# Gate product on GpSimd, second normalization on ScalarE as scale and bias

## The chip, the cores and the metric

The kernel runs on one core of one Trainium2 chip. The metric is device time in microseconds (us). Before the change it is 3508.47 us, the median of three runs (3508.07 to 3510.55).

A core has several engines, each with its own in-order instruction queue: TensorE (PE in the profile; its weight loads are listed as PEld), VectorE (DVE), ScalarE (ACT), GpSimd (POOL) and SyncE (SP), which here only issues DMAs. They meet only at semaphores. SBUF is the on-chip memory, PSUM the small memory that TensorE writes to.

## What is computed

The input x has 8 batches of 2048 positions with 512 channels, all in 32-bit floats. Cut to what matters:

```python
def _layernorm(x, axis=-1, eps=1e-05):
    m = jnp.mean(x, axis=axis, keepdims=True)
    v = jnp.var(x, axis=axis, keepdims=True)
    return (x - m) / jnp.sqrt(v + eps)

def attn(x):                       # a gated long convolution
    proj = (x @ in_proj_w + in_proj_b).reshape(B, L, C, 3)
    v = short_conv(proj[..., 0]) + short_b
    h = coefs(pos)                 # a small network gives the filter, as long as the sequence
    conv = irfft(rfft(v, n=2 * L) * rfft(h, n=2 * L), n=2 * L)[:, :L]
    return (proj[..., 2] * conv) @ out_w + out_b

def ffn(x):                        # 8 chosen adapters, mixed
    return einsum('k,kod,bsd->bso', weights, W[ids], x) + einsum('k,ko->o', weights, b[ids])

x = x + attn(_layernorm(x))
x = x + ffn(_layernorm(x))
```

The reference loops over two convolution branches, but only the last one reaches the output, so the kernel computes that one.

## The kernel before, in words

The Fourier transform over a sequence is split in two: across the 128 partitions it is a matrix product with a table, and across the 16 positions that a partition holds it is a second, small product. This gives three stages.

1. The first stage (lines 330 to 382) normalizes x, projects it to v and to the gate x2, transforms v across the partitions and stores both to DRAM. The adapters are mixed and the filter is built (lines 175 to 327) between its batches.
2. The middle stage (lines 385 to 440) goes over 32 groups of frequencies: it finishes the transform, multiplies by the filter and starts the way back. GpSimd adds the complex products at lines 426 and 427.
3. The last stage (lines 443 to 501) is where the change lies. It loops over 8 groups n of two position rows and, inside, over 8 batches b: 64 iterations, with two tiles t of 128 x 512 in each.

One iteration of the last stage, with the line of each step:

- SP loads zt (460, the transformed convolution), x2 (462, the gate; its tile is named x2t) and xt (464, the block's input). Each has three buffers.
- For each of the two tiles, GpSimd makes cor (468 and 469, a correction term, two instructions) and xb (471, the input plus the output bias). TensorE ends the inverse transform in ps_y (474, two matmuls). VectorE adds cor (479) and multiplies by the gate (480), both into gt. TensorE transposes gt in four pieces (166), ScalarE copies the result to gT (167), TensorE projects it with out_w into ps_o (171, four matmuls), and VectorE adds xb and has x1 (485).
- `layer_norm_stats` (144 to 153) makes mean and 1/sd of both tiles: two bn_stats (148), two bn_aggr (150), one Sqrt on ScalarE (152), one reciprocal (153). `normalized` (155 to 160) makes xn1 on VectorE, one instruction for each tile, subtracting the mean and multiplying by 1/sd (157).
- For each tile, TensorE transposes xn1 (166), ScalarE copies it to xn1T (167), GpSimd adds the adapters' bias to x1 for x1b (495), TensorE projects with mixed_wT (171) and VectorE adds x1b into ot (498). GpSimd issues the store of both (499).

Because helpers record their own lines, L166, L167 and L171 each stand for two places; the tile names tell them apart. In the timeline xn1 appears as xn, and x1 as x. Each 32-bit matmul leaves two records in the trace.

The source order is not the order of the queues. The tile framework's scheduler fixes each engine's order when the kernel is built, taking an instruction when its inputs and a free buffer are there. The tiles gt, gT, cor, xb, x1, xn1, xn1T, x1b and ot have two buffers each, the pools ps_x and ps_y two banks each and ps_o four. So the stage is pipelined over iterations. In the trace TensorE's steady order is: the adapter projection of one iteration, the transposes of gt and the output projection of the next, the ps_y of a still later one, and then the transposes of xn1. VectorE has, in the steady state: ot for the first tile, ot for the second, two of L479, two of L480, then x1, bn_stats and bn_aggr for each tile, the reciprocal, two of L157. GpSimd has: the store's issue, four cor instructions, then x1b, xb, x1b, xb.

Of the kernel before, what the change touches and what calls it, by code (L numbers as in the profile page):

```python
# [25 lines left out]
F32 = mybir.dt.float32  # L26
I32 = mybir.dt.int32
AF = mybir.ActivationFunctionType
ALU = mybir.AluOpType
# [3 lines left out]
P = 128  # L33
# [38 lines left out]
def block_kernel(  # L72
# [24 lines left out]
    nc = tc.nc  # L97
# [46 lines left out]
    def layer_norm_stats(pool, xt, to, n):  # L144

        bn = pool.tile([P, n, 6], F32, name="bn")
        for t in range(n):
            nc.vector.bn_stats(bn[:, t, :], xt[:, t, :])  # L148
        for t in range(n):
            nc.vector.bn_aggr(to[:, t, :], bn[:, t, :])  # L150
        sd = pool.tile([P, n], F32, name="sd")
        nc.scalar.activation(sd, to[:, :, 1], AF.Sqrt, bias=eps)  # L152
        nc.vector.reciprocal(to[:, :, 1], sd)  # L153

    def normalized(xn, xt, st, n):
        for t in range(n):
            nc.vector.tensor_scalar(  # L157
                xn[:, t, :], xt[:, t, :], st[:, t, 0:1], st[:, t, 1:2],
                ALU.subtract, ALU.mult,
            )  # L160

    def transposed(psum, src, to):

        ps = psum.tile([P, CC, P], F32, name="ps_t")
        for cc in range(CC):
            nc.tensor.transpose(ps[:, cc, :], src[:, ts(cc, P)], ident)  # L166
        nc.scalar.copy(to, ps)  # L167

    def projected(ps, xT, w):
        for kc in range(CC):  # L170
            nc.tensor.matmul(  # L171
                ps, lhsT=xT[:, kc, :], rhs=w[:, kc, :], start=(kc == 0), stop=(kc == CC - 1)
            )
# [156 lines left out]
    NR = 4  # L330
    with tc.tile_pool(name="vw", bufs=1) as vw, tc.tile_pool(
        name="vin", bufs=3
    ) as vin, tc.tile_pool(name="v2", bufs=2) as v2, tc.tile_pool(
        name="ps_a", bufs=2, space=PSUM
    ) as ps_a, tc.tile_pool(name="ps_b", bufs=3, space=PSUM) as ps_b, tc.tile_pool(
        name="ps_c", bufs=3, space=PSUM
# [13 lines left out]
        for b in range(B):  # L350
# [4 lines left out]
            for n in range(R // NR):  # L355
# [6 lines left out]
                x2 = v2.tile([P, NR, C], F32, name="x2")  # L362
# [23 lines left out]
    with tc.tile_pool(name="mt", bufs=3) as mt, tc.tile_pool(name="mh", bufs=2) as mh, tc.tile_pool(  # L386
        name="my", bufs=3
    ) as my, tc.tile_pool(name="ps_v", bufs=2, space=PSUM) as ps_v, tc.tile_pool(
        name="ps_z", bufs=4, space=PSUM
# [53 lines left out]
    NR = 2  # L443
    with tc.tile_pool(name="ofix", bufs=2) as ofix, tc.tile_pool(
        name="oin", bufs=3
    ) as oin, tc.tile_pool(name="o2", bufs=2) as o2, tc.tile_pool(
        name="ps_x", bufs=2, space=PSUM
    ) as ps_x, tc.tile_pool(name="ps_y", bufs=2, space=PSUM) as ps_y, tc.tile_pool(
        name="ps_o", bufs=4, space=PSUM
    ) as ps_o:  # L450
        ow_s = ofix.tile([P, CC, C], F32, name="ow_s", bufs=1)
        nc.sync.dma_start(ow_s, out_w.rearrange("(kc p) c -> p kc c", p=P))
        v0_b = ofix.tile([P, B, C], F32, name="v0_b", bufs=1)
        nc.sync.dma_start(v0_b, v0_d.partition_broadcast(P))
        for n in range(R // NR):
            fix = ofix.tile([P, 2, NR, C], F32, name="fix2")
            nc.sync.dma_start(fix, fix_d[:, :, ts(n, NR), :].rearrange("k p r c -> p k r c"))
            for b in range(B):
                zt = oin.tile([P, NR, 2, C], F32, name="zt")
                nc.sync.dma_start(zt, z_d[b, :, ts(n, NR), :, :])  # L460
                x2 = oin.tile([P, NR, C], F32, name="x2t")
                nc.sync.dma_start(x2, x2_d[b, :, ts(n, NR), :])
                xt = oin.tile([P, NR, C], F32, name="xt3")
                nc.sync.dma_start(xt, x[b].rearrange("(p r) c -> p r c", r=R)[:, ts(n, NR), :])
                x1 = o2.tile([P, NR, C], F32, name="x1")
                for t in range(NR):
                    cor = o2.tile([P, C], F32, name="cor")
                    nc.gpsimd.tensor_tensor(cor, fix[:, 0, t, :], v0_b[:, b, :], ALU.mult)
                    nc.gpsimd.tensor_tensor(cor, cor, fix[:, 1, t, :], ALU.add)
                    xb = o2.tile([P, C], F32, name="xb")  # L470
                    nc.gpsimd.tensor_tensor(xb, xt[:, t, :], out_bb, ALU.add)
                    ps = ps_y.tile([P, C], F32, name="ps_y")
                    for i in range(2):
                        nc.tensor.matmul(  # L474
                            ps, lhsT=last[:, i, :], rhs=zt[:, t, i, :],
                            start=(i == 0), stop=(i == 1),
                        )
                    gt = o2.tile([P, C], F32, name="gt")
                    nc.vector.tensor_tensor(gt, ps, cor, ALU.add)  # L479
                    nc.vector.tensor_tensor(gt, gt, x2[:, t, :], ALU.mult)  # L480
                    gT = o2.tile([P, CC, P], F32, name="gT")
                    transposed(ps_x, gt, gT)
                    ps = ps_o.tile([P, C], F32, name="ps_o")
                    projected(ps, gT, ow_s)
                    nc.vector.tensor_tensor(x1[:, t, :], ps, xb, ALU.add)  # L485
                st1 = o2.tile([P, NR, 2], F32, name="st1")
                layer_norm_stats(o2, x1, st1, NR)
                xn1 = o2.tile([P, NR, C], F32, name="xn1")
                normalized(xn1, x1, st1, NR)
                ot = o2.tile([P, NR, C], F32, name="ot")  # L490
                for t in range(NR):
                    xn1T = o2.tile([P, CC, P], F32, name="xn1T")
                    transposed(ps_x, xn1[:, t, :], xn1T)
                    x1b = o2.tile([P, C], F32, name="x1b")
                    nc.gpsimd.tensor_tensor(x1b, x1[:, t, :], mixed_bb, ALU.add)  # L495
                    ps = ps_o.tile([P, C], F32, name="ps_o")
                    projected(ps, xn1T, mixed_wT)
                    nc.vector.tensor_tensor(ot[:, t, :], ps, x1b, ALU.add)  # L498
                nc.gpsimd.dma_start(  # L499
                    out[b].rearrange("(p r) c -> p r c", r=R)[:, ts(n, NR), :], ot  # L500
                )
# [53 lines left out]
```

## Time and profile before

| | |
|---|---|
| median of three runs | 3508.47 us |
| the profiled execution's own time | 3511.88 us |
| its span, first to last instruction | 3510.1 us |
| mean granted TensorE clock | 0.974 |
| PE busy in the span | 3152.2 us (90%) |
| DVE busy | 1636.5 us (47%) |
| POOL busy | 1119.1 us (32%) |
| ACT busy | 592.7 us (17%) |
| last stage, first cor to the end | about 2110 to 3510 us |

A line of a group in the profile reads: source line, engine, operation, tile written <- tiles read, shapes, count | busy us in total, mean ns of one | idle us of the engine before it, and what released it. A line of the timeline reads: start in us, length in us, engine, line, operation, tiles, count of merged instructions, and in brackets the idle time before it with its releaser. A matmul's end is modelled; its start is recorded.

Over 200 us from the middle of the last stage (2800 to 3000 us), PE was busy 180.72 us, DVE 128.64, POOL 99.17 and ACT 24.33.

### The profile page before, as it was taken

How to read it: one execution, taken by the hardware profiler on the slowest of the kernel's cores; microseconds unless marked ns; L12 is line 12 of the kernel's file. 1: busy time of each engine (PE TensorE's matmuls, PEld its weight loads, DVE VectorE, ACT ScalarE, POOL GpSimd, SP SyncE). 2: the span in 40 equal slices, each digit the busy share in tenths (PEclk: the TensorE clock that was granted, in tenths of full speed). 3: DMA queues.
4: the chain of work that ended last, by engine and by line, in shares of the span. 5: the costliest groups of instructions: out<-in, count | busy, mean ns of one | idle time of the engine just before them, and what ended most of it. 6: DMA issues, size and time to landing. Idle time of an engine off the chain costs nothing. (4 is left out here: it accounts for less than half of the span.)

```text
span 3510.1 us, 25679 instructions
## 1 busy us (share of the span) xinstructions
PE 3152.2 (90%) x9142; PEld 1338.9 (38%) x9142; DVE 1636.5 (47%) x2225; ACT 592.7 (17%) x1110; POOL 1119.1 (32%) x934
## 2 busy tenths in 40 slices
PE   7999679999999998888888868999899999999997
PEld 3443124444444443222222214444444444444443
DVE  6222642222222211444444435666666666666663
ACT  1212111111111111222222221111111111111111
POOL 0000840000000000444444435455544444455542
PEclk9998669999999999999999999999999999999999
DMA  7322232223222223666666645333333333333330
GB/s 268 123 107 90 102 120 114 111 111 120 114 115 107 102 96 125 225 214 213 216 218 216 214 174 215 132 123 135 120 133 126 140 123 132 120 137 121 120 108 24
DMA packets 156119, 493.54 MB, mean 141 GB/s; under 512 B 11783, under 2 KB 16200, under 8 KB 139481
## 3 DMA queue, kind: packets, MB, share of 16 engines
q1 hardware_dynamic: 88312, 304.46, 24.8%
q10 hardware_dynamic: 56160, 145.50, 10.9%
q0 software_dynamic: 11520, 41.95, 3.0%
q8 instruction: 73, 1.20, 0.1%
q14 instruction: 54, 0.43, 0.0%
HBM read 273.75 MB, written 218.12 MB: 140 GB/s over the span
## 5 line engine op out<-in xcount | busy, mean ns | idle before, releaser
L426 POOL TENSOR_TENSOR y<-m 128x512 f32<-128x512 f32 x128 | 162.2, 1267 | 1288.5 <-DMA hs<-sh_d 917.9
L171 PE MATMUL ps_p<-wv_s,xnT 128*128 128x512 f32 x1024 | 469.9, 602 | 18.0 <-ACT xnT L167 18.0
L171 PE MATMUL ps_o<-ow_s,gT 128*128 128x512 f32 x1024 | 456.8, 599 | 18.7 <-ACT gT L167 18.7
L171 PE MATMUL ps_p<-wx_s,xnT 128*128 128x512 f32 x1024 | 460.3, 592 | 0.0
L171 PE MATMUL ps_o<-mixed_wT,xn1T 128*128 128x512 f32 x1024 | 454.6, 597 | 0.0
L432 PE MATMUL ps_z<-y,tab 64*128 64x512 f32 x1024 | 290.4, 644 | 89.3 <-POOL y L426 72.5
L480 DVE TENSOR_TENSOR gt<-gt,x2t 128x512 f32<-128x512 f32 x128 | 364.6, 2885 | 0.1
L370 DVE TENSOR_TENSOR v<-ps_p,bv_b 128x512 f32<-128x512 f32 x128 | 88.5, 691 | 468.6 <-PE ps_p L171 468.6
L378 ACT COPY s<-ps_s 128x512 f32<-128x512 f32 x256 | 149.9, 585 | 917.7 <-PE ps_s L377 917.7
L498 DVE TENSOR_TENSOR ot<-ps_o,x1b 128x512 f32<-128x512 f32 x128 | 88.6, 692 | 459.3 <-issue 273.5
L415 PE MATMUL ps_v<-s,tab 128*64 128x512 f32 x1024 | 280.8, 598 | 10.2 <-PE ps_v L415 10.2
L171 PEld LDWEIGHTS ps_p<-wx_s,xnT 128*128 128x128 f32 x1024 | 194.6, 190 | 244.9 <-issue 244.9
L171 PEld LDWEIGHTS ps_p<-wv_s,xnT 128*128 128x128 f32 x1024 | 190.3, 191 | 248.9 <-issue 215.3
L171 PEld LDWEIGHTS ps_o<-ow_s,gT 128*128 128x128 f32 x1024 | 189.2, 190 | 248.9 <-issue 213.8
L171 PEld LDWEIGHTS ps_o<-mixed_wT,xn1T 128*128 128x128 f32 x1024 | 191.3, 192 | 218.0 <-issue 217.4
L166 PE MATMUL ps_t<-ident,xn 128*128 128x128 f32 x1024 | 150.4, 281 | 128.1 <-DVE xn L157 127.9
L474 PE MATMUL ps_y<-zt,last 128*128 128x512 f32 x512 | 233.6, 599 | 21.2 <-DMA zt<-z_d 21.2
L377 PE MATMUL ps_s<-v,first 128*128 128x512 f32 x512 | 240.8, 592 | 0.0
L499 POOL DMA_DIRECT2D out<-ot x64 | 38.1, 595 | 585.1 <-DVE ot L498 585.1
L437 ACT COPY z<-ps_z 128x512 f32<-128x512 f32 x256 | 137.5, 589 | 505.5 <-PE ps_z L432 505.5
L421 DVE TENSOR_TENSOR m<-ps_v,h 128x512 f32<-128x512 f32 x128 | 87.9, 686 | 276.7 <-PE ps_v L415 276.7
L373 DVE TENSOR_TENSOR x<-ps_p,bx_b 128x512 f32<-128x512 f32 x128 | 88.4, 690 | 265.0 <-PE ps_p L171 264.5
(89 smaller groups left out, 3102.4 us busy)
## 6 DMA issues: line engine op xcount, KB each, us to landing
s_d<-s ACTq DMA_DIRECT2D x128, 512.0 KB
s<-s_d SPq DMA_DIRECT2D x64, 1024.0 KB
z_d<-z ACTq DMA_DIRECT2D x64, 1024.0 KB
zt<-z_d SPq DMA_DIRECT2D x64, 1024.0 KB
xt<-in_x SPq DMA_DIRECT2D x32, 1024.0 KB
x_d<-x SPq DMA_DIRECT2D x32, 1024.0 KB
x2t<-x_d SPq DMA_DIRECT2D x64, 512.0 KB
xt<-in_x SPq DMA_DIRECT2D x64, 512.0 KB
```

Of the source, the lines that this page charges most:

```text
L166: nc.tensor.transpose(ps[:, cc, :], src[:, ts(cc, P)], ident)
L171: nc.tensor.matmul(ps, lhsT=xT[:, kc, :], rhs=w[:, kc, :], start=(kc == 0), stop=(kc == CC - 1))
L370: nc.vector.tensor_tensor(v, ps, bv_b, ALU.add)
L377: nc.tensor.matmul(ps, lhsT=first[:, i, :], rhs=v, start=True, stop=True)
L378: nc.scalar.copy(s[:, i, :], ps)
L415: nc.tensor.matmul(ps[i][a * 64 : a * 64 + 64, :], lhsT=tab[:, ts(i, 64)], rhs=s[:, 2 * w + a, :], start=True, stop=True,)
L426: nc.gpsimd.tensor_tensor(y[:, 0, :], m[:, 0, :], m[:, 1, :], ALU.subtract)
L432: nc.tensor.matmul(pz[a], lhsT=tab[rows, ds(128 + 128 * i, P)], rhs=y[rows, i, :], start=(i == 0), stop=(i == 1),)
L437: nc.scalar.copy(z[:, 2 * w + a, :], pz[a])
L474: nc.tensor.matmul(ps, lhsT=last[:, i, :], rhs=zt[:, t, i, :], start=(i == 0), stop=(i == 1),)
L480: nc.vector.tensor_tensor(gt, gt, x2[:, t, :], ALU.mult)
L498: nc.vector.tensor_tensor(ot[:, t, :], ps, x1b, ALU.add)
```

## The change

The gate product of L480 is issued on GpSimd instead of VectorE, with the same operands. The call of `normalized` in the last stage is replaced: VectorE computes nb, which is minus mean times 1/sd, for both tiles in one instruction on [128, 2] operands, and ScalarE makes xn1 as Identity(x1 * scale + bias), with 1/sd as scale and nb as bias, one instruction for each tile. The first stage's normalization stays on VectorE.

```diff
                     gt = o2.tile([P, C], F32, name="gt")
                     nc.vector.tensor_tensor(gt, ps, cor, ALU.add)
-                    nc.vector.tensor_tensor(gt, gt, x2[:, t, :], ALU.mult)
+                    nc.gpsimd.tensor_tensor(gt, gt, x2[:, t, :], ALU.mult)
                     gT = o2.tile([P, CC, P], F32, name="gT")
...
                 xn1 = o2.tile([P, NR, C], F32, name="xn1")
-                normalized(xn1, x1, st1, NR)
+
+                nb = o2.tile([P, NR], F32, name="nb")
+                nc.vector.scalar_tensor_tensor(
+                    nb, st1[:, :, 0], -1.0, st1[:, :, 1], ALU.mult, ALU.mult
+                )
+                for t in range(NR):
+                    nc.scalar.activation(
+                        xn1[:, t, :], x1[:, t, :], AF.Identity, bias=nb[:, t : t + 1],
+                        scale=st1[:, t, 1:2],
+                    )
                 ot = o2.tile([P, NR, C], F32, name="ot")
```

## The prediction, made before the result was known

> **What bounds the kernel now.** I read the page's first part (PE busy 90% of the span), then the costliest groups for what PE waits for, then the timeline of one steady iteration of the last stage, engine by engine.
>
> From the groups, the gate product and the transposes of the normalized tiles (the last line covers the first stage too; in the list of waits, 106.9 of the 127.9 us fall between 2120 and 3470 us):
>
> ```profile
> L480 DVE TENSOR_TENSOR gt<-gt,x2t 128x512 f32<-128x512 f32 x128 | 364.6, 2885 | 0.1
> L166 PE MATMUL ps_t<-ident,xn 128*128 128x128 f32 x1024 | 150.4, 281 | 128.1 <-DVE xn L157 127.9
> ```
>
> TensorE's timeline over one iteration:
>
> ```profile
> 2812.52 7.13 PE L171 MATMUL ps_o<-ow_s,gT 128*128 128x512 f32 x16 [0.29 <-ACT gT L167]
> 2819.49 3.60 PE L474 MATMUL ps_y<-zt,last 128*128 128x512 f32 x8
> 2823.98 0.63 PE L166 MATMUL ps_t<-ident,xn 128*128 128x128 f32 x4 [0.89 <-DVE xn L157]
> 2825.39 0.63 PE L166 MATMUL ps_t<-ident,xn 128*128 128x128 f32 x4 [0.78 <-DVE xn L157]
> 2825.85 7.03 PE L171 MATMUL ps_o<-mixed_wT,xn1T 128*128 128x512 f32 x16
> ```
>
> The next transposes of gt start at 2832.72, those of this iteration started at 2811.19: a period of 21.53 us, of which PE idles 0.29 + 0.89 + 0.78 = 1.96. All but the 0.29 is waiting for VectorE's normalization. That is the only place where the last stage can be shortened without taking matmuls away: at most 1.67 us an iteration, 107 us in 64.
>
> VectorE and GpSimd in the same iteration:
>
> ```profile
> 2813.27 5.88 DVE L480 TENSOR_TENSOR gt<-gt,x2t 128x512 f32<-128x512 f32 x2
> 2819.07 0.68 DVE L485 TENSOR_TENSOR x<-ps_o,xb 128x512 f32<-128x512 f32 x1
> 2820.61 0.67 DVE L485 TENSOR_TENSOR x<-ps_o,xb 128x512 f32<-128x512 f32 x1
> 2822.59 0.17 DVE L153 RECIPROCAL st<-sd 128x2 f32<-128x2 f32 x1 [0.36 <-ACT sd L152]
> 2822.80 2.44 DVE L157 TENSOR_SCALAR xn<-x,st 128x512 f32<-128x512 f32 x2
> ```
>
> ```profile
> 2812.45 0.59 POOL L499 DMA_DIRECT2D out<-ot  x1 [9.02 <-DVE ot L498]
> 2813.07 2.49 POOL L468 TENSOR_TENSOR cor<-fix,v_b 128x512 f32<-128x512 f32 x2
> 2815.52 2.47 POOL L469 TENSOR_TENSOR cor<-cor,fix 128x512 f32<-128x512 f32 x2
> 2819.83 1.27 POOL L495 TENSOR_TENSOR x1b<-x,mixed_bb 128x512 f32<-128x512 f32 x1 [1.84 <-DVE x L485]
> 2823.50 1.45 POOL L471 TENSOR_TENSOR xb<-xt,out_bb 128x512 f32<-128x512 f32 x1
> ```
>
> The gate product is the thing to look at. Its least duration is 0.675 us, but the first of each pair took 5.28 (2813.27 to 2818.55) and the second about 0.6. GpSimd's four cor instructions ran from 2813.07 to 2817.99: a VectorE instruction with both inputs in SBUF stood still until GpSimd's whole run was over, then took 0.56. VectorE's additions with one input in PSUM (0.68), the statistics (0.69) and the reciprocal (0.17) show no such wait beside a busy GpSimd.
>
> **Part one: the gate product leaves VectorE.** Its 5.88 us go. They delayed the first x1 to 2819.07, although its half of the projection was done near 2816.0 (half of the 6.97 us from 2812.52); with its statistics it then pushed the second x1 to 2820.61, 1.1 us after the projection's end at 2819.49. Without it the second x1 starts one hop after that end. The chain that ended last has this hop and the rest undisturbed: PE ends 3465.39, DVE x starts 3465.48, the reciprocal ends 3467.66, so 2.18 us from x1 to the reciprocal's end. In the shown iteration: 2819.49 + 0.09 + 2.18 = 2821.76, where it was 2822.76. Gain: 1.0 us of the chain.
>
> On GpSimd it costs two instructions of 1.225 us (the spacing of cor: 2813.07 to 2814.30). The Trainium skill (GPSIMD Engine Reference, § Engine selection) speaks against it: elementwise with two inputs is about twice as slow there. The row agrees on the ratio (1.225 against 0.675) but that isn't what decides: by the rule the move loses 2 x 0.55 us, by the row it takes 5.88 us off VectorE and needs 2.45 of GpSimd, which idles about 9 us before each store. The product's result is not needed before the next transposes of gt at 2832.72, so the 2.45 us lie beside other work: nothing on the path directly. Queued behind it on GpSimd are cor (needed 20 us later), x1b (needed near 2829) and xb (needed an iteration later): all have slack. SP's reload of x2t starts earlier (its buffer is free at 2815.5, not 2819.15); the reload of xt, and zt behind it, starts 0.4 us later, with three buffers each. I cost these at nothing.
>
> What it does change is GpSimd's run. All its work of an iteration becomes ready near 2813 or soon after: two products, four cor, and x1b and xb twice, whose x1 now come at about 2816.7 and 2820.3. Ten instructions of 1.225 us from 2813.07 end at 2825.35, without a gap, where before there was a pause from 2817.99 to 2819.83. The order among the ten doesn't change this, unless one whose x1 is still missing is placed too early; cor stood ahead of x1b before, which speaks against that.
>
> **Part two: nb.** This is one tiny VectorE instruction, and it has two SBUF inputs. The trace has no tiny one of this kind. From below it is bounded by the reciprocal on 128x2, 0.17 us; from above by the gate product, waiting until GpSimd's run ends. It would be ready at 2821.79, in the middle of the new run. Both ways of waiting are in this trace. In the filter stage (L310 has two SBUF inputs as well) and in the last stage's first iteration:
>
> ```profile
> 423.44 1.74 DVE L310 TENSOR_TENSOR g<-hp,w_b 128x512 f32<-128x512 f32 x1 [1.15 <-POOL g L312]
> 429.99 4.17 DVE L310 TENSOR_TENSOR g<-hp,w_b 128x512 f32<-128x512 f32 x1 [1.48 <-POOL g L312]
> 2124.64 1.76 DVE L480 TENSOR_TENSOR gt<-gt,x2t 128x512 f32<-128x512 f32 x1
> ```
>
> The 1.7 us cases waited for one GpSimd instruction and then got in; the 4.17 us case sat out three. What tells them apart in the timeline: where GpSimd's run followed directly on a DMA that GpSimd issued (the store before cor; the filter's store before the run at 428.68), VectorE got in only when the run was over. Where GpSimd had stood idle for another engine (421.84), or had issued no DMA (2124.64), it got in after one. The new run follows directly on the store's issue at 2812.45, just as the cor run does. So I take the upper end: nb ends about 0.1 us after the run, at 2825.45, instead of 2821.97.
>
> Here the Trainium skill differs from the row: SBUF — State Buffer, § Who interferes with whom and the summary's last rows, says that a VectorE instruction with two SBUF inputs contends with a reading GpSimd instruction, and that the second to issue blocks until the first finishes. By the rule nb waits for one instruction, to 2822.87 (2813.07 + 8 x 1.225); by L480's row, to 2825.35. I go with the row, as it has the same predecessor in the queue; the rule is my first rival.
>
> **Part three: normalization on ScalarE.** It removes two L157 (1.03 and 1.49 us, slowed by GpSimd; 2.44 together) and adds two ACTIVATEs. The nearest row is L267, 128x512 with one pointer operand from PSUM: 687 ns, against 585 for the plain copy, so about 0.10 for a pointer; with two, 0.79. The bounds are 0.585 and 0.82 (with 0.03 for an SBUF source: L152's 295 ns plus 510 elements at the skill's 0.833 ns gives 0.72 with one pointer). I take 0.80, and 0.71 for the second's spacing, an estimate from ScalarE: Activation LUTs, § What ACT_TABLE_LOAD costs. Its § Table sets says identity is in every set, so Sqrt needs no reload; no Identity is in this trace, and two reloads at the trace's 1.283 us would add 160 us. ScalarE was idle here, but in its queue the copies to xn1T now stand behind both ACTIVATEs, and these wait for nb.
>
> **The sum.** xn1 first tile: 2825.49 to 2826.29; second ends 2827.00. First transposes 0.15 later (2826.44), their copy 0.72 after that (2827.16, as 2823.98 to 2824.70) for 0.58, to 2827.74; second transposes at 2827.15, done by 2827.61. The adapter projection starts at 2827.80, against 2825.85: 1.95 us later. The rest of the period (8.30 before 2819.49, 6.87 after) stays, and the run is anchored to the store, so it repeats. Of 64 iterations some 62 are in the steady state: 62 x 1.95 = 121 us. On the profiled execution (3511.9) that is 3633; it lies 3.4 above the median, so on the median 3508.5 + 121 = 3630. With 0.585 us for xn1 the shift is 1.75 us (3617); with a slower nb and 0.82, some 2.2 (3645).
>
> **The rivals.**
> *One-instruction wait (the skill's rule).* The longer run lets VectorE in after the current instruction. nb ends at 2822.97; xn1 at 2823.81 and 2824.52; copy 2824.68 to 2825.26; projection at 2825.31, 0.54 us earlier than now: 62 x 0.54 = 33, so 3475, faster. The point of decision is the end of nb at 2823.5: later than that, the stage gets slower. For it: the rows of 1.74 and 1.76. Against it: 5.28 in nearly every iteration behind the same store. A scheduler's order with a gap in GpSimd's run leads here too.
> *nb isn't held at all,* two elements being too short to matter. nb ends 2821.97, xn1 2822.81 and 2823.52; then ps_y's modelled end (2823.09) and the second ACTIVATE bound the transposes (2823.10, 2823.66), the copy runs 2823.82 to 2824.40, projection at 2824.45: 1.40 x 62 = 87, so 3421. For it: the tiny reciprocal and bn_aggr run freely beside GpSimd. Against it: they have one input.
> *Another order of the queues* (transposes of the next gt put into the gap, or xn1's ahead of ps_y): somewhere between 3421 and 3650.
>
> **The numbers.** Held to the end of the run 0.62; one instruction 0.18; not held 0.12; another order 0.08, half of it to either side. Predicted 3630. Its own range is 3610 to 3645. The range for all reaches to the first rival: 3465 to 3650. A measurement of this kernel tells about 0.2% (7 us) from no change: faster 0.33, same 0.03, slower 0.64.
>
> **What would show it.** Right: nb's mean near 3.5 us, ending just after xb; GpSimd's ten instructions unbroken behind the store; PE's wait before the transposes up from 1.67 to about 3.6 us, now for ACT xn; a period near 23.5. Wrong: nb at 0.2 us or 1 to 1.5; a pause in GpSimd's run; ACT table loads in the loop; another order on PE.

## The result and the profile after

After the change the kernel takes 3723.99 us (median of 4 runs, 3723.35 to 3726.67), against 3509.51 us before in the same comparison: 1.061 times as long, 95% interval 1.059 to 1.063. The direction of the forecast and its mechanism on VectorE and GpSimd held; the amount did not: 214 us more where 121 were forecast, above the range.

From the page of the changed kernel, TensorE's busy time and three groups (line, operation, tiles, count | busy us, mean ns | idle before, releaser):

```profile
PE 3269.3 (88%) x9142; PEld 1407.9 (38%) x9142; DVE 1343.3 (36%) x2033; ACT 689.7 (19%) x1238; POOL 1260.0 (34%) x1062
L171 PE MATMUL ps_o<-mixed_wT,xn1T 128*128 128x512 f32 x1024 | 535.0, 682 | 0.0
L166 PE MATMUL ps_t<-ident,xn 128*128 128x128 f32 x1024 | 189.3, 340 | 220.3 <-ACT xn L495 201.2
L491 DVE SCALAR_TENSOR_TENSOR nb<-st 128x2 f32<-128x2 f32 x64 | 208.9, 3265 | 2.2
```

nb, two elements a partition, takes 3265 ns on average. TensorE's wait before the transposes is now for ScalarE's xn. And two rows that the forecast left alone have grown: the adapter projection's matmuls from 597 to 682 ns, the transposes of xn (first and last stage together) from 281 to 340. The projection's row in the kernel before:

```profile
L171 PE MATMUL ps_o<-mixed_wT,xn1T 128*128 128x512 f32 x1024 | 454.6, 597 | 0.0
```

One steady iteration, GpSimd's timeline:

```profile
2817.06 0.59 POOL L508 DMA_DIRECT2D out<-ot  x1 [11.82 <-DVE ot L507]
2817.68 2.49 POOL L480 TENSOR_TENSOR gt<-gt,x2t 128x512 f32<-128x512 f32 x2
2820.13 2.48 POOL L468 TENSOR_TENSOR cor<-fix,v_b 128x512 f32<-128x512 f32 x2
2822.58 2.48 POOL L469 TENSOR_TENSOR cor<-cor,fix 128x512 f32<-128x512 f32 x2
2825.03 1.25 POOL L504 TENSOR_TENSOR x1b<-x,mixed_bb 128x512 f32<-128x512 f32 x1
2826.25 1.25 POOL L471 TENSOR_TENSOR xb<-xt,out_bb 128x512 f32<-128x512 f32 x1
2827.47 1.25 POOL L504 TENSOR_TENSOR x1b<-x,mixed_bb 128x512 f32<-128x512 f32 x1
2828.69 1.25 POOL L471 TENSOR_TENSOR xb<-xt,out_bb 128x512 f32<-128x512 f32 x1
```

Ten instructions stand directly behind the store and run without a pause to 2829.94. VectorE and ScalarE beside them:

```profile
2826.38 0.17 DVE L153 RECIPROCAL st<-sd 128x2 f32<-128x2 f32 x1 [0.36 <-ACT sd L152]
2826.58 3.39 DVE L491 SCALAR_TENSOR_TENSOR nb<-st 128x2 f32<-128x2 f32 x1
```

```profile
2830.00 1.52 ACT L495 ACTIVATE xn<-x,nb,st 128x512 f32<-128x512 f32 x2 [3.65 <-DVE nb L491]
```

nb is ready at 2826.58 and ends at 2829.97, just after GpSimd's run. The reciprocal beside the same run takes its 0.17 us. So the engines do not meet only at semaphores: nb needs nothing that this run of GpSimd makes, and yet it stands still until the run is over. TensorE follows, and then the granted clock in three stretches of its work (a stretch and its length in us; the busy time and count of PE, PEld, DVE, ACT and POOL; then the clock, the DMA share and GB/s):

```profile
2824.11 3.60 PE L474 MATMUL ps_y<-zt,last 128*128 128x512 f32 x8
2830.87 1.97 PE L166 MATMUL ps_t<-ident,xn 128*128 128x128 f32 x8 [3.16 <-ACT xn L495]
2832.71 7.75 PE L171 MATMUL ps_o<-mixed_wT,xn1T 128*128 128x512 f32 x16
2840.30 1.04 PE L166 MATMUL ps_t<-ident,gt 128*128 128x128 f32 x8
```

```profile
2830.87:2832.71 1.84, 1.84 (x8) 1.56 (x8) 0.00 (x0) 1.23 (x2) 0.00 (x0) 0.50 0.90 276
2832.71:2836.50 3.79, 3.79 (x9) 1.84 (x9) 0.00 (x0) 0.59 (x1) 0.00 (x0) 0.83 0.67 281
2836.50:2840.30 3.80, 3.80 (x10) 1.60 (x9) 0.69 (x1) 0.00 (x0) 0.00 (x0) 1.00 0.00 0
```

TensorE stands still for 3.16 us, and when it goes on, its clock is at half (0.50) through the transposes and into the projection, then full again. That second effect is what the forecast lacked.

### The profile page after: what moved, and what is told of

It reads as the page before. It is cut to its first block, busy times and chain, and to the rows that moved or that the text cites. A ratio compares the mean times of both kernels' runs of the same rounds, so it can differ in the third digit from the quotient of the medians.

```text
span 3722.8 us, 25873 instructions
## 1 busy us (share of the span) xinstructions
PE 3269.3 (88%) x9142; PEld 1407.9 (38%) x9142; DVE 1343.3 (36%) x2033; ACT 689.7 (19%) x1238; POOL 1260.0 (34%) x1062
## 4 chain that ended last, share of the span: by engine, by line
PE 68%; DVE 13%; POOL 10%; ACT 5%; issue 3%; DMA 1%; DVEq 0%; POOLq 0%; SPq 0%; ACTq 0%
PE ps_o L171 26%; PE ps_p L171 24%; PE ps_s L377 6%; DVE nb L491 6%; POOL y L426 4%; PE ps_t L166 4%; POOL y L427 4%; PE ps_v L415 3%; PE ps_z L432 2%; ACT xn L495 2%; DVE m L423 1%; PE ps_v L400 1%; DVE x L485 1%; DVE bn L148 1%; ACT gT L167 1%
## 5 line engine op out<-in xcount | busy, mean ns | idle before, releaser
L171 PE MATMUL ps_o<-mixed_wT,xn1T 128*128 128x512 f32 x1024 | 535.0, 682 | 0.0
L166 PE MATMUL ps_t<-ident,xn 128*128 128x128 f32 x1024 | 189.3, 340 | 220.3 <-ACT xn L495 201.2
L171 PEld LDWEIGHTS ps_o<-mixed_wT,xn1T 128*128 128x128 f32 x1024 | 224.8, 227 | 274.0 <-issue 262.4
L166 PEld LDWEIGHTS ps_t<-ident,xn 128*128 128x128 f32 x1024 | 151.1, 174 | 313.9 <-ACT xn L495 260.7
L491 DVE SCALAR_TENSOR_TENSOR nb<-st 128x2 f32<-128x2 f32 x64 | 208.9, 3265 | 2.2
L485 DVE TENSOR_TENSOR x<-ps_o,xb 128x512 f32<-128x512 f32 x128 | 88.6, 692 | 309.2 <-PE ps_o L171 309.2
```

Of the source, the lines that this page charges most:

```text
L171: nc.tensor.matmul(ps, lhsT=xT[:, kc, :], rhs=w[:, kc, :], start=(kc == 0), stop=(kc == CC - 1))
L491: nc.vector.scalar_tensor_tensor(nb, st1[:, :, 0], -1.0, st1[:, :, 1], ALU.mult, ALU.mult)
```

## The experiments

Ten runs, each timed against the kernel before on the same chip. Two questions: what decides how long nb is held, and what the rest of the loss is.

### Only the gate product moved

```diff
-                    nc.vector.tensor_tensor(gt, gt, x2[:, t, :], ALU.mult)
+                    nc.gpsimd.tensor_tensor(gt, gt, x2[:, t, :], ALU.mult)
```

> Only the gate product goes to GpSimd; the normalization stays on VectorE (two L157, one SBUF input each[...]). Theory (behind its own store GpSimd's unbroken run keeps VectorE off the shared port until the run ends, whatever kind of instruction asks): the first L157 is ready near 0.3 us after ps_y's second matmul and sits out the run, about 3.5 us; L157's mean near 2 us, TensorE's pause near 2.8 us, projection 1.35 us later than before: 3595, up to 3660 if the clock falls as well. Rival ([...]after one GpSimd instruction, as L157 does in the kernel before, 1.03 and 1.49 us): the projection starts 0.9 us earlier than before, 3455.

Measured: 3671.43 us, ratio 1.046 (1.044 to 1.048). This half alone loses 160 us. VectorE's two L157, then TensorE, then the clock from there on:

```profile
2852.20 4.12 DVE L157 TENSOR_SCALAR xn<-x,st 128x512 f32<-128x512 f32 x2
```

```profile
2856.01 1.69 PE L166 MATMUL ps_t<-ident,xn 128*128 128x128 f32 x8 [2.68 <-DVE xn L157]
```

```profile
2856.01:2857.57 1.56, 1.56 (x8) 1.28 (x9) 0.31 (x1) 0.58 (x1) 0.00 (x0) 0.59 0.55 97
2857.57:2865.58 8.01, 8.01 (x17) 3.58 (x17) 0.69 (x1) 0.58 (x1) 0.00 (x0) 0.87 0.43 177
```

The first L157 alone took 3.66 us, until just after GpSimd's run (2855.86 against 2855.57); the second, with the run over, 0.53. So it isn't only instructions with two SBUF inputs that are held: in the kernel before, behind GpSimd's pause, the same two took 1.03 and 1.49, getting in after one GpSimd instruction each. The theory gave 3595, or up to 3660 if the clock fell as well. It fell, at a pause of 2.68 us, and the time lies a little above that upper figure.

### Only the normalization moved

```diff
-                    nc.gpsimd.tensor_tensor(gt, gt, x2[:, t, :], ALU.mult)
+                    nc.vector.tensor_tensor(gt, gt, x2[:, t, :], ALU.mult)
```

(against the changed kernel)

> Only the normalization goes to ScalarE, with nb as in the change; the gate product stays on VectorE. GpSimd then pauses before x1b as in the kernel before, so nb meets a run that begins behind a pause. Theory (the run's beginning decides): nb waits for one GpSimd instruction, near 0.9 us, projection 0.15 us later than before: about 3520. Rival (an instruction with two SBUF inputs always waits for the end of the run): nb 2.2 us, projection 1.55 us later, 3605. Second rival (nb never gets held by a run that does not follow the store): nb 0.2 us, 3480.

Measured: 3519.24 us, ratio 1.0026 (1.0015 to 1.0037), as the theory had it. GpSimd's x1b, VectorE's nb and TensorE's transposes in one iteration:

```profile
2864.36 1.27 POOL L504 TENSOR_TENSOR x1b<-x,mixed_bb 128x512 f32<-128x512 f32 x1 [1.84 <-DVE x L485]
```

```profile
2867.32 0.77 DVE L491 SCALAR_TENSOR_TENSOR nb<-st 128x2 f32<-128x2 f32 x1
```

```profile
2868.99 1.36 PE L166 MATMUL ps_t<-ident,xn 128*128 128x128 f32 x8 [1.38 <-ACT xn L495]
```

Here GpSimd pauses 1.84 us before x1b. nb becomes ready within the second x1b (2866.81 to 2868.07) and ends with it: one instruction, not the run. TensorE's pause is 1.38 us and its transposes keep their length (1.36, where they took 1.97 after the change): no clock loss in this iteration. It isn't quite safe, though: before the stage's last iterations the granted clock fell three times, for 3.41 us each. One of them, in the columns of the section before:

```profile
2305.92:2309.33 3.41, 3.41 (x6) 1.35 (x5) 0.00 (x0) 0.10 (x1) 0.00 (x0) 0.50 0.98 395
```

### The whole change, nb without a second SBUF input

```diff
-                nc.vector.scalar_tensor_tensor(
-                    nb, st1[:, :, 0], -1.0, st1[:, :, 1], ALU.mult, ALU.mult
-                )
+                for t in range(NR):
+                    nc.vector.tensor_scalar(
+                        nb[:, t : t + 1], st1[:, t, 0:1], st1[:, t, 1:2], -1.0,
+                        ALU.mult, ALU.mult,
+                    )
```

> The whole change, but nb is made by two instructions of one element a partition, with 1/sd as a pointer scalar, so that each has a single SBUF tensor input. Theory (the second SBUF input is what is held): both run in about 0.17 us beside the busy GpSimd, TensorE's pause before the transposes is near nothing, its clock stays at 1.00, period about 20.3 us: 3433. Rival (any VectorE instruction between statistics and ScalarE is held, or a pointer scalar counts as a second input): 3.4 us for the first, time as with the whole change, 3724.

Measured: 3428.68 us, ratio 0.977 (0.975 to 0.979). The group of nb, VectorE's timeline and TensorE's:

```profile
L492 DVE TENSOR_SCALAR nb<-st 128x1 f32<-128x1 f32 x128 | 21.4, 209 | 2.2
```

```profile
2858.32 0.34 DVE L492 TENSOR_SCALAR nb<-st 128x1 f32<-128x1 f32 x2
```

```profile
2859.44 1.36 PE L166 MATMUL ps_t<-ident,xn 128*128 128x128 f32 x8
2860.82 7.13 PE L171 MATMUL ps_o<-mixed_wT,xn1T 128*128 128x512 f32 x16
```

The same arithmetic on the same two numbers, with 1/sd read as a pointer scalar (one number for each partition), isn't held although GpSimd's run is as long as after the change. TensorE has no pause before the transposes. One wait of 3.4 us, with the fall of the clock that comes with it, is thus worth the whole distance from 3724 to 3429. What frees this form isn't separated: it has one SBUF tensor input, and it handles one element instead of two. One tensor input alone isn't enough, since L157, the same operation with one tensor input, was held at 512 elements.

### The store moved to SyncE

```diff
-                nc.gpsimd.dma_start(
+                nc.sync.dma_start(
                     out[b].rearrange("(p r) c -> p r c", r=R)[:, ts(n, NR), :], ot
                 )
```

> The whole change, with the output store issued by SyncE instead of GpSimd. GpSimd's ten instructions of an iteration stay, but no store stands ahead of them. Theory (the store at the head of the run is what makes nb wait to the end): nb waits for at most one instruction, 0.2 to 1.3 us, TensorE's pause is under 1.6 us, its clock stays near 1.00: 3475 with 1.2 us for nb, 3430 with 0.2. Rival (an unbroken run of any beginning holds nb to its end): nb 3.4 us, 3724.

Measured: 3464.93 us, ratio 0.987 (0.985 to 0.988); nb 836 ns on average. But taking the store out also gave GpSimd another order, with one addition directly behind its product and a pause of 0.08 us there. The next two runs take these apart.

### No store ahead, and no pause inside

```diff
+                cors = []
                 for t in range(NR):
                     cor = o2.tile([P, C], F32, name="cor")
                     nc.gpsimd.tensor_tensor(cor, fix[:, 0, t, :], v0_b[:, b, :], ALU.mult)
-                    nc.gpsimd.tensor_tensor(cor, cor, fix[:, 1, t, :], ALU.add)
+                    cors.append(cor)
+                for t in range(NR):
+                    nc.gpsimd.tensor_tensor(cors[t], cors[t], fix[:, 1, t, :], ALU.add)
```

> As the run before it with the store on SyncE, and the four cor instructions written so that no addition stands directly behind the product it needs: GpSimd's ten instructions then have no pause among them, and no store ahead. Theory A (the store at the head of the run decides): nb near 0.8 us as with the store on SyncE, 3465. Theory B (a pause of 0.08 us inside the run decides, which that order had between 2857.66 and 2857.74): nb 3.4 us, about 3720.

Measured: 3458.54 us, ratio 0.985 (0.984 to 0.987); nb 716 ns on average. The run's first instruction, the one in which nb becomes ready, and nb:

```profile
2848.64 1.26 POOL L485 TENSOR_TENSOR gt<-gt,x2t 128x512 f32<-128x512 f32 x1 [8.47 <-DVE gt L484]
2857.22 1.26 POOL L476 TENSOR_TENSOR xb<-xt,out_bb 128x512 f32<-128x512 f32 x1
```

```profile
2857.78 0.72 DVE L496 SCALAR_TENSOR_TENSOR nb<-st 128x2 f32<-128x2 f32 x1
```

GpSimd's ten instructions run from 2848.64 to 2860.93 without a pause, and nb ends with the one in progress (2858.48). An unbroken run that begins behind GpSimd's idling does not hold nb beyond one instruction. Theory A holds for this run.

### A store ahead, and a pause inside

```diff
+                cor2 = o2.tile([P, NR, C], F32, name="cor", bufs=1)
+                nc.gpsimd.tensor_tensor(
+                    cor2, fix[:, 0, :, :], v0_b[:, b : b + 1, :].to_broadcast([P, NR, C]),
+                    ALU.mult,
+                )
+                nc.gpsimd.tensor_tensor(cor2, cor2, fix[:, 1, :, :], ALU.add)
```

> The whole change with the store left on GpSimd, and cor of both tiles made by one product and one addition of twice the length, so that the addition waits for the product inside the run: a pause of some 0.08 us behind the store. GpSimd's work stays about the same. Theory A (the store at the head decides, up to the run's end): nb 3.4 us, about 3720. Theory B (any pause inside the run lets VectorE in afterwards): nb at most 1.3 us, 3430 to 3475.

Measured: 3466.34 us, ratio 0.987 (0.985 to 0.989). Theory A falls, as it was put. GpSimd, then VectorE:

```profile
2849.68 0.60 POOL L512 DMA_DIRECT2D out<-ot  x1 [8.09 <-DVE ot L511]
2850.30 2.49 POOL L484 TENSOR_TENSOR gt<-gt,x2t 128x512 f32<-128x512 f32 x2
2852.76 2.34 POOL L467 TENSOR_TENSOR cor<-fix,v_b 128x1024 f32<-128x1024 f32 x1
2855.17 2.35 POOL L471 TENSOR_TENSOR cor<-cor,fix 128x1024 f32<-128x1024 f32 x1
```

```profile
2859.19 0.79 DVE L495 SCALAR_TENSOR_TENSOR nb<-st 128x2 f32<-128x2 f32 x1
```

The product ends at 2855.10, the addition starts at 2855.17, and four more instructions follow without a pause until 2862.42. nb comes at 2859.19 and gets in after the one in progress (which ends at 2859.97). So in these runs the long hold needs both: a DMA issued by GpSimd directly ahead, and no pause since. A pause as short as this one ended it. (The pause came with instructions of twice the length, which no run takes apart from it. But in the filter stage of the kernel before, a pause of 0.62 us behind such a DMA went with a wait for one instruction of ordinary length: the 1.74 us of L310 in the prediction.)

### Filling TensorE's pause

```diff
+                ps = ps_d.tile([P, C], F32, name="ps_d")
+                nc.tensor.matmul(
+                    ps[:, 0 : 2 * NR], lhsT=ident, rhs=st1.rearrange("p n k -> p (n k)"),
+                    start=True, stop=True,
+                )
+                for _ in range(3):
+                    nc.tensor.matmul(ps, lhsT=ident, rhs=x1[:, 0, :], start=True, stop=True)
```

(behind nb in the changed kernel; ps_o has three banks)

> The whole change plus work that is thrown away: in each iteration one small and three full matmuls into a spare PSUM bank (ps_o gives up one of its four), ready once the statistics are. TensorE's order puts one ps_y matmul behind the transposes, so the projection starts near 8.8 us after the output projection's end. Theory (TensorE's clock falls to half because it pauses for over 3 us): the pause is cut to about 1.5 us, the granted clock stays near 1.00 and the stage gets faster although it has 2.6 us more to do: period 24.0, about 3660. Rival (transposes and projection are slow behind the pause because loads and ScalarE's copies crowd that moment): clock still 0.94, time 3735 or more.

Measured: 3662.69 us, ratio 1.043 (1.042 to 1.045), against 1.061 for the change: more work, less time. nb is held as before. TensorE's timeline, and 900 us of the stage:

```profile
2870.83 2.82 PE L500 MATMUL ps_d<-x,ident 128*128 128x512 f32 x6
2874.85 1.36 PE L166 MATMUL ps_t<-ident,xn 128*128 128x128 f32 x8 [1.20 <-ACT xn L502]
```

```profile
2400.00:3300.00 900.00, 842.05 (x2402) 393.35 (x2401) 347.57 (x451) 151.22 (x261) 483.09 (x414) 1.00 0.34 116
```

With the pause cut to 1.20 us the granted clock is 1.00; the changed kernel's was 0.91 over the same 900 us. The transposes are back at 1.36 us. The pause made the clock fall, not the crowding of loads and copies behind it.

### The kernel before, with the store on SyncE

The edit is that of the store above, made in the kernel before.

> The kernel before, with only the store moved from GpSimd to SyncE. Theory (the store at the head of GpSimd's run, or the unbroken run, holds the gate product): the first gate product takes 1.2 to 1.9 us instead of 5.28, the first x1 no longer waits for it, the second x1 starts one hop after its projection, about 1.0 us earlier, and the projection of the adapters 0.8 us earlier: 3460. Rival (GpSimd's four cor instructions hold it whatever stands ahead of them): 5.3 us again, 3510.

Measured: 3438.83 us, ratio 0.980 (0.978 to 0.981). VectorE's gate product:

```profile
2858.99 3.05 DVE L480 TENSOR_TENSOR gt<-gt,x2t 128x512 f32<-128x512 f32 x2
```

The pair takes 3.05 us instead of 5.88: one word in the store's line removes most of the hold in the kernel before. Here too GpSimd's order changed with it, to one addition directly behind its product and a pause of 0.07 us (2859.82 to 2859.89), so this run alone does not say which of the two freed the gate product. The gain was 73 us, more than the 50 expected: the first L157 was done before ps_y ended, and only the second made TensorE wait (0.78).

### Two more, for the parts' prices

Only the normalization moved, with nb by pointer scalars:

> Only the normalization goes to ScalarE, with nb by pointer scalars (one SBUF tensor input each); the gate product stays on VectorE and is held behind the store as in the kernel before. This prices the gate product's hold alone. nb is free (0.34 us for both), but the second x1 still starts 1.0 us late, so the projection is about 0.4 us earlier than before: 3485. If the gate product's hold costs nothing beside TensorE's queue: 3429, as with both parts moved.

Measured: 3478.79 us, ratio 0.990 (0.989 to 0.992). The whole change with nb by pointer scalars and the store on SyncE:

> The whole change with nb by pointer scalars, and the store on SyncE as well. If nothing on VectorE asks for the shared port any more, the store's place is of no weight: 3429, within 0.2%. If something is still held behind the store (or a pointer read is), it gets faster: 3415.

Measured: 3426.36 us, ratio 0.975 (0.974 to 0.977): level with the version that keeps the store on GpSimd (3428.68). So the gate product's move is worth some 50 us (3478.79 to 3428.68) once nb isn't held. These two are the fastest kernels of the study; with the pointer scalar the change's idea gains 2.3%.

## Why the prediction was wrong in size

**Part one, right.** The gate product's move does what was worked out: the ten GpSimd instructions run unbroken for 12.26 us (12.25 forecast) behind the store. The second x1 starts 0.27 us behind the start of ps_y, where 0.09 was taken: that hop was read from a modelled end of matmuls, and then set behind the start of the next ones, which is 0.16 earlier (2819.49 against 2812.52 + 7.13). It cost the forecast nothing, since nb waits for GpSimd.

**Part two, right.** nb ends 5.86 us after the output projection's end (2829.97 less 2824.11); 5.96 was forecast. The choice of L480's row over the Trainium skill's rule was right here: by the rule of SBUF — State Buffer, § Who interferes with whom and the summary's row on both engines, nb would have waited for one instruction, as it does behind a pause (0.77 us), and the kernel would have come to 3475 by the prediction's sum. The rule describes the runs behind a pause; behind a store of GpSimd's own it is off by the rest of the run. The prediction put the condition as following "directly on the store's issue". The runs confirm it and add that a pause since then lifted it wherever one was seen (0.07, 0.62 and 1.84 us).

**Part three, right.** The ACTIVATE took 806 ns (0.80 forecast), the pair 1.52 us (1.51), with no table load in the loop.

**The sum, wrong in one term.** It said: "The rest of the period (8.30 before 2819.49, 6.87 after) stays". The 8.30 stayed (2815.80 to 2824.11 is 8.31); what lies behind the pause did not. The transposes of both tiles took 1.97 us, where they take 1.36 at full clock, and from the projection's start to the next transposes it was 7.59 us in the shown iteration, where 6.87 were taken. In three periods that follow one another, the transposes of gt start at 2915.39, 2941.29, 2965.99 and 2990.48: 25.90, 24.70 and 24.49 us, against 23.48 forecast. The prediction even wrote that TensorE's wait would rise to "about 3.6 us" (it was 3.16) and did not ask what a pause of that length does to the engine that pauses: it put TensorE's clock behind the pause at full, without a reason.

The trace shows what it does. Here are the stretches from the pause on, cut where the granted clock changes (the first covers 3.41 us up to the fall):

```profile
2827.17:2830.58 3.41, 0.53 (x2) 0.00 (x0) 2.79 (x1) 0.58 (x1) 2.77 (x3) 1.00 0.00 0
2830.58:2833.99 3.41, 3.12 (x10) 2.33 (x11) 0.00 (x0) 2.11 (x4) 0.00 (x0) 0.50 0.88 315
2833.99:2854.47 20.48, 17.91 (x47) 7.95 (x46) 9.28 (x12) 1.37 (x3) 12.86 (x11) 1.00 0.36 127
2854.47:2861.30 6.83, 5.93 (x13) 3.42 (x14) 0.00 (x0) 2.69 (x4) 0.00 (x0) 0.50 0.62 233
2861.30:2881.78 20.48, 17.02 (x48) 7.73 (x46) 9.28 (x12) 2.75 (x5) 12.86 (x11) 1.00 0.18 55
2881.78:2885.19 3.41, 3.37 (x9) 1.91 (x8) 0.00 (x0) 1.31 (x3) 0.00 (x0) 0.50 0.99 399
```

The clock falls at 2830.58, still inside the pause (TensorE goes on at 2830.87), behind 3.41 us in which TensorE worked for 0.53 and no DMA moved. And the clock changes in steps: half for 3.41, 6.83 and 3.41 us, full for 20.48 between them, which is 1, 2, 1 and 6 times 3.41. One round, three stretches at half clock and three at full, is 75.09 us, 22 steps, and so is the sum of the three periods above. The long periods, of 25.90 us, are those with two steps in a row at half, as from 2854.47 on: where the pause falls among the steps makes the difference. The Trainium skill's page TensorE: Matmul & The Clock Gate, § Part 1, describes such free-running windows of 3413 ns, and a clock that goes to half after an idle one. The step agrees. The idle window does not: by that rule a pause of 3.16 us, which fills no window, would have left the clock full, and the kernel some 100 us faster (an estimate, from the next paragraph).

How much each took is an estimate. In the run with the filled pause, at full clock, the copy of the first tile ends 8.10 us after the output projection (2876.19 less 2868.09), so the adapter projection could start near 8.15, against 6.36 before: 1.79 us, times 63 periods 113 us, near the 121 forecast. The mean period, from the first store's issue to the last, went from (3502.1 - 2143.1) / 63 = 21.57 us to (3714.8 - 2142.2) / 63 = 24.96: 3.39 us, times 63 = 214 us. The rest, about 100 us, is the clock. The pages give a similar split: TensorE's wait before the transposes rose by 92 us (128.1 to 220.3), and the same 9142 records kept it busy for 117 us more (3152.2 to 3269.3).

**The rivals.** The one-instruction wait was put at 3475; runs in which nb waits so came to 3458.54, 3464.93 and 3466.34. nb not held was put at 3421; with a second small instruction it came to 3428.68. Another order of TensorE's queue didn't occur.

**Open.** Why a DMA issued on GpSimd makes the following run shut VectorE out until a pause isn't shown. The expectations suppose a port that both engines share; the trace has no view of one, nor of what GpSimd does inside an instruction. What frees the one-element form of nb, and not L157, is open too. Nor was it settled how little TensorE may work in a step of 3.41 us before the clock falls.

## What to carry to other kernels

Before giving GpSimd more work, look at which VectorE instructions then fall within its run, and compare them with instructions that the trace shows held there: a two-element instruction can cost as much as the run has left. On a chain that TensorE waits for, try a small instruction with one tensor and a pointer scalar, and try issuing the DMA ahead of a long GpSimd run from another engine. When a forecast lengthens TensorE's pause, forecast its clock as well, and charge for the matmuls behind the pause: here some 1.6 us for each (the 100 us over 63 periods).

## What the runs showed that was not expected

- In the steady state the clock fell to half in every iteration at recorded pauses of 3.16 us (after) and 2.68 us (0.59 over the transposes, with only the gate product moved). Before the stage's last iterations it fell three times at 1.38 us (only the normalization moved), once in the kernel before (pauses of 1.26 and 0.78 us there, mostly 0.89 and 0.78), and not at all at 1.20 us (the filled pause).
- An instruction with one SBUF tensor input, L157 on 128x512, was held to the run's end too: 3.66 us behind the store, 1.03 and 1.49 behind a pause. Statistics, reciprocal and the one-element pointer-scalar form of nb were not held.
- A pause of 0.07 us in GpSimd's run was enough to bring nb's hold from 3.39 to 0.79 us.
